# A DiT block on one core: keys loaded a group earlier, pairs of projection tiles leaving PSUM together, bias rows loaded at once, a longer lag behind the reciprocals

## The chip, the cores and the metric

The kernel runs on one core of one Trainium2 chip. The metric is the time of the program on the device in microseconds (us), as the median of several runs. The data type is float32 throughout.

## The reference

One block of a diffusion transformer with adaptive layer norm, for a batch of 2 sequences of 2048 tokens with 576 channels, 16 heads of 36 channels, and an MLP of 2304 hidden channels:

```
ada = silu(c) @ W_ada + b_ada                       # c (2, 576), W_ada (576, 3456)
shift_msa, scale_msa, gate_msa, shift_mlp, scale_mlp, gate_mlp = split(ada, 6)
h = layernorm(x) * (1 + scale_msa) + shift_msa      # x (2, 2048, 576)
q, k, v = split(h @ W_qkv + b_qkv, 3)               # W_qkv (576, 1728)
o = softmax(q * 36**-0.5 @ k.T) @ v                 # for each of the 16 heads
x = x + gate_msa * (o @ W_proj + b_proj)
h = layernorm(x) * (1 + scale_mlp) + shift_mlp
x = x + gate_mlp * (gelu_tanh(h @ W_fc1 + b_fc1) @ W_fc2 + b_fc2)
```

## The kernel before

The program has three stages: a front that makes queries, keys and values for all tokens; a loop over the attention of 8 blocks (a block is 512 queries of one sequence) times 16 heads, into which the projection and the MLP of earlier blocks are laid; and an end that finishes the projection and MLP of the last block. 576 channels are five pieces of the contraction, four of 128 and one of 64.

**The front** (up to L580). `load_ada` fetches the weights of one of the six parts of `ada`; `rows_of` (L408) multiplies them with the conditioning into two rows, and `modulation` (L428) turns these rows into columns, by five small matmuls, and adds 1 to the scales with three VectorE operations. For each of the 8 groups of 512 tokens, `queries_keys_values` (L206) loads four x tiles, normalizes them on VectorE, transposes them on TensorE, and applies scale and shift into `hT`. Then it makes the nine column tiles of 128 queries and keys. Two column tiles, a pair, share one PSUM tile `pq` of two banks (`wide`, of which there are three), one bank for each half, and the ninth is alone. The eviction `kept` (L255) adds the bias, on ScalarE for the first four column tiles and on VectorE for the others, and SP (SyncE's queue) stores the tile `ev` to `qk_d` in DRAM. In a pair it comes directly after the matmuls of its half. The values `pv` go through VectorE (`vt`, L342) and SP to `v_d`. The front's steps are generators; a second generator, `later` (L502), is advanced between them. It makes the two gates `g1` and `g2`, multiplies two bias rows of each sequence with them (tile `row`, L519 to L526, results in `gb_d` and `gp_d`), and multiplies the weights of the projection and of fc2 with them (`gated`: POOL loads at L480, VectorE multiplies at L493, POOL stores at L499).

**The loop.** A unit is one head of one block; there are 128. Its 2048 keys are taken in four groups, one to a slot of the loop, which has 512 slots. The work of one unit is spread over many slots, since scores run 8 slots ahead of the weighing (`AHEAD`):

- `load_keys` (L160): four SP loads, of keys `kT` (36 rows, twice) and queries `qT` (twice), at partitions 0 and 64; L169 and L170 issue them.
- `scores` (L625) on TensorE; `keep` (L638) copies them from PSUM to `e` on ScalarE; `maxima` (L643) folds them into `acc` on VectorE.
- After the fourth group, `turn` (L661) transposes the maxima on TensorE into the PSUM buffers that scores use; `across` reduces them (L671, `mx`), and SP stores them to `m_d` (L672) and loads them back broadcast over all partitions as `m` (L675).
- `less` (L680) subtracts `m` on VectorE, `exps` (L684) exponentiates on ScalarE, and `weigh` (L696) multiplies with the values `v` on TensorE. `load_values` (L600) fetches `v` with one SP load after a small VectorE memset.
- `take` (L708, L709) adds the two halves of the result into `up`; `store` sends it to `o_d` and `sum_d`: SP writes one half (L715, L716), POOL adds the other with accumulating DMAs (L717, L718).

In slot G the loop body issues, in this order: key and value loads, scores and copies, a filling, exponentials, transposes, the weighing, reductions and subtractions, and the stores of the unit that finished in the slot before. The loads are placed by these two conditions, in which `sg` and `g` are the group numbers of the scores' and the weighing's unit:

```
            if sg == 1 and su + 1 < NU:
                units[su + 1].load_keys()
            if g == 1 and -1 <= u and u + 1 < NU:
                units[u + 1].load_values()
```

With these, SP's order for one unit is m_d, m, o_d, sum_d, kT, qT, kT, qT, v.

A filling is a piece of work of an earlier block, chosen by a running account of cost. When a block's 16 heads are stored, its generators are queued: `gather` and `block`. `gather` (L1018) loads the sums and the outputs `oT` on POOL, takes the reciprocals of the sums and stores them to `rec_d` on POOL (L1040), then goes through KC + 2 steps: in step kc it loads the reciprocals of piece kc, broadcast over the rows of each head, by four or five SP loads (`r`, L1051) for each of the first four pieces, and multiplies piece kc - 2 of `oT` (L1059). `block` does the projection (`po`, L776), the residual, the second layer norm, fc1 (`pf`, L1147), gelu (L1158) and fc2 (`py`, L1195), whose result is added into `x_b` (L1207). A helper at L104 records the matmuls of the last contraction piece of 64 (`quads`), whatever the tile.

**The end** (L1365 to L1381) runs what is left after the last slot: each turn takes a filling and then calls `advance()` twice, which advances the gather of the last block by one step each time.

[...] SP's queue and ScalarE's queue issue hardware DMAs, POOL's issues software DMAs. The built program gives eight semaphores to SP's and ScalarE's transfers in turn, so that each issue also waits for the one eight before it.

Of the kernel before, what the change touches and what calls it, by code (L numbers as in the profile page):

```python
# [10 lines left out]
F32 = mybir.dt.float32  # L11
# [6 lines left out]
P = 128  # L18
# [4 lines left out]
def dit_block_kernel(  # L23
# [150 lines left out]
    with ExitStack() as front:  # L174
# [32 lines left out]
        def queries_keys_values(b, tb):  # L207
            mvs = lnp.tile([P, TB, nc.vector.BN_AGGR_DIM], F32, tag="mv", name=f"mv_{b}_{tb}", bufs=2)
            xts, xns = [], []
            for i in range(TB):  # L210
                xt = lnp.tile([P, C], F32, tag="xt", name=f"xt_{b}_{tb}_{i}", bufs=8)
                by = nc.sync if (b, tb) in ((0, 0), (0, 1)) else nc.scalar
                seq(by.dma_start(out=xt, in_=x[b, ts(tb * TB + i, P), :]))
                xts.append(xt)
            yield
# [52 lines left out]
            for m in range(0, NQK, 2):  # L268
                pq = wide(f"pq_{b}_{tb}_{m}")
                two = m + 1 < NQK  # L270
                for r in range(2):

                    cols, at = (ts(m + r, P), slice(None)) if two else (ts(m, P), ts(r, QB // 2))
                    n = QB if two else QB // 2
                    for kc in range(KC - 1):
                        seq(
                            nc.tensor.matmul(  # L277
                                pq[:, r, :n],
                                lhsT=w_in[:, kc, cols],
                                rhs=hT[:, kc, at],  # L280
                                start=(kc == 0 and not (two and r)),
                                stop=(kc == KC - 2 and two and r == 1),
                            )
                        )
                    if two and r == 0:
                        quads(
                            [pq[:, i, :] for i in range(2)],
                            [w_in[ts(i, 64), KC - 1, ts(m + i, P)] for i in range(2)],
                            tail,
                            (False, True),  # L290
                        )
                    if two:
                        kept(m + r, pq[:, r, :])
                        yield
                if not two:
                    quads(
                        [pq[:, i, :n] for i in range(2)],
                        [w_in[ts(i, 64), KC - 1, ts(m, P)] for i in range(2)],
                        [tail[i][:, ts(i, n)] for i in range(2)],
                        (False, False),  # L300
                    )
                    kept(m, pq[:, :, :n])
                    if tb == NQB - 1:
                        first_keys.extend(load_keys(0))
                    yield
# [91 lines left out]
            seq(nc.tensor.transpose(pt[:, ts(kc, B)], c_in[:, ts(kc, P)], ident[:B, :B]))  # L397
        cT = ap.tile([P, KC, B], F32, name="cT")
        seq(nc.vector.tensor_copy(cT.rearrange("p k b -> p (k b)"), pt[:, 0 : KC * B]))
        pt = bank("pt_bias")  # L400
        nb = NQK + NF
        seq(nc.tensor.transpose(pt[:, 0:nb], b_in, ident[:nb, :nb]))
        nq = C // P
        seq(nc.vector.tensor_scalar_mul(bias[:, 0:nq], pt[:, 0:nq], SCALE))
        seq(nc.vector.tensor_scalar_mul(bias[:, nq : nq + 1], pt[:, nq : nq + 1], qscale))
        seq(nc.vector.tensor_copy(bias[:, nq + 1 : nb], pt[:, nq + 1 : nb]))

        def rows_of(part):  # L408

            wa = was.pop(part)  # L410
# [17 lines left out]
        def modulation(part, t):  # L428

            pm = pms.pop(0) if pms else wide(f"pm_{part}")[:, 0, :]  # L430
            if part == 0:
                pms.append(pm[:, KC * B :])
            for fc in range(KC):
                m = P if fc < KC - 1 else KL
                seq(
                    nc.tensor.matmul(
                        pm[:m, ts(fc, B)], lhsT=t[:, ds(fc * P, m)], rhs=of_b, start=True, stop=True
                    )
                )
            to = 2 * (part // 3) + (1 - part % 3)  # L440
            add = 1.0 if part % 3 == 1 else 0.0
            spans = [(0, P, 0, KC - 1), (0, KL, KC - 1, KC), (64, KL, KC - 1, KC)]
            for at, m, lo, hi in spans:
                seq(
                    nc.vector.tensor_scalar_add(
                        mod[at : at + m, to, lo:hi, :].rearrange("p k b -> p (k b)"),
                        pm[:m, lo * B : hi * B],
                        add,
                    )
                )  # L450

        def gates(part, made):

# [48 lines left out]
        def later():  # L502

            was[2] = load_ada(2)
            was[5] = load_ada(5)
            yield
            yield
            yield
# [10 lines left out]
            half = [ap.tile([P, C], F32, name=f"half_{b}") for b in range(B)]  # L519
            for b in range(B):  # L520
                seq(nc.vector.tensor_scalar_mul(half[b], g2[b], 0.5))
                for to, src, g in ((gb_d, b_fc2, g2), (gp_d, b_proj, g1)):
                    r = ap.tile([1, C], F32, tag="row", name=f"row_{b}", bufs=2)
                    seq(nc.gpsimd.dma_start(out=r, in_=src.unsqueeze(0)))
                    seq(nc.vector.tensor_mul(r, r, g[b][0:1, :]))
                    seq(nc.gpsimd.dma_start(out=to[b].unsqueeze(0), in_=r))  # L526
            yield
            split = lambda w: [
                (pieces(w)[0][:, kc : kc + 2, :], P, 2) for kc in range(0, KC - 1, 2)
# [14 lines left out]
            t = rows_of(3)  # L544
            pas[4] = cleared(4)
            yield
            modulation(3, t)
            t = rows_of(4)
            yield
            modulation(4, t)  # L550

        next(stages[0])
        ts_ = [rows_of(part) for part in range(2)]
        next(stages[0])
        for part in range(2):
            modulation(part, ts_[part])
        for b in range(B):
            seq(nc.vector.tensor_copy(spread[b], of_b[:, b : b + 1].to_broadcast([P, P])))
        rest = later()
# [16 lines left out]
    with ExitStack() as main_part:  # L576
# [444 lines left out]
        def gather(k):  # L1021
# [18 lines left out]
            seq(nc.gpsimd.dma_start(out=flat_rows(rec_d[k]), in_=sums))  # L1040
            yield
            recs = []
            for kc in range(KC + 2):
                if kc < KC:
                    r = xp.tile([P, CP], F32, tag="xn", name=f"r_{k}_{kc}")[:, :QB]
                    for to in (0,) if kc < KC - 1 else (0, 64):
                        f, end = kc * P, min(kc * P + P, C)
                        while f < end:
                            n = min(D - f % D, end - f)
                            seq(  # L1050
                                nc.sync.dma_start(  # L1051
                                    out=r[ds(to + f - kc * P, n), :],
                                    in_=rec_d[k][f // D, :].partition_broadcast(n),
                                )
                            )
                            f += n
                    recs.append(r)
                if kc >= 2:
                    seq(nc.vector.tensor_mul(oT[:, kc - 2, :], oT[:, kc - 2, :], recs[kc - 2]))  # L1059
                yield  # L1060

        begun = {}
# [244 lines left out]
        for G in range(-AHEAD, NU * NG + 1):  # L1307
# [1 line left out]
            state["slot"] = G  # L1309

            su, sg = divmod(G + AHEAD, NG)
            if sg == 1 and su + 1 < NU:
                units[su + 1].load_keys()
            if g == 1 and -1 <= u and u + 1 < NU:
                units[u + 1].load_values()
            cu, cg = divmod(G - 1 + AHEAD, NG)
            chain = cg == NG - 1 and 0 <= cu < NU
# [50 lines left out]
        while work:  # L1368
# [8 lines left out]
                dones.append(lights.pop(0)()[1])  # L1377
            for done in dones:
                done()
            advance()  # L1380
            advance()  # L1381


# [43 lines left out]
```

## Time and profile before

| what | value |
|---|---|
| three runs | 3772.09, 3773.57, 3774.59 us; median 3773.57 |
| profiled execution, its own time | 3765.39 us |
| its span | 3763.6 us |
| granted TensorE clock, mean | 0.995 |
| PE (TensorE) busy | 3706.8 us |
| DVE (VectorE) busy | 2950.2 us |
| ACT (ScalarE) busy | 2331.1 us |
| POOL (GpSimd) busy | 617.1 us |
| moved by DMA | 382.11 MB, mean 102 GB/s |
| front, 0 to 262 us: PE busy | 232.6 us |
| loop, 262 to 3500 us: PE busy | 3219.6 us |
| end, 3500 to 3763.6 us: PE busy | 254.6 us |

The span is the time from the first to the last instruction of the profiled execution; its own time is 1.8 us more. In a row of waits, "PE s L625 <- DMA qT<-qk_d: 10.7, 5, 5.0" says that TensorE, before instructions of line 625 that write tile s, stood idle for 10.7 us in 5 places, at most 5.0 us at once, and that a DMA into qT from qk_d ended the wait. A row of the timeline has the start and the duration in us, the engine, the line, the operation, the tiles with partitions x elements, a count, and in brackets the idle time before it with what ended it. "SPq" and "DVEq" are the parts of an engine that issue transfers. The granted clock is the share of TensorE's full clock that the chip's throttle allowed.

### The profile page before, as it was taken

The numbers are of one execution on the slowest core, as the hardware profiler recorded it, in microseconds if no ns is written. First come the engines' busy times: TensorE is split into PE (matmuls) and PEld (weight loads), VectorE is DVE, ScalarE is ACT, GpSimd is POOL, SyncE is SP. The second block draws the span as 40 slices with busy tenths as digits, with TensorE's granted clock in tenths as the row PEclk, the third lists the DMA queues.
The fourth block names the chain that finished last, engine by engine and source line by source line (L and its number), as shares of the span: only waits on it lengthen the run. The fifth ranks groups of instructions, "written<-read, shape, count | busy, mean of one in ns | idle before, by whom it ended". The sixth has DMA issues, their size and how long they took to land. (4 is left out here: it accounts for less than half of the span.)

```text
span 3763.6 us, 59194 instructions
## 1 busy us (share of the span) xinstructions
PE 3706.8 (98%) x23926; PEld 1727.1 (46%) x23926; DVE 2950.2 (78%) x3002; ACT 2331.1 (62%) x2164; POOL 617.1 (16%) x868
## 2 busy tenths in 40 slices
PE   8999999999999999999999999999999999999999
PEld 4454443534444534444444444444445444444465
DVE  4626889879888888898889888988889888988322
ACT  0005777668776686667677767767766766676321
POOL 0201111221111121211121112111121112111211
PEclk9999999999999999999999999999999999999999
DMA  6823444454435353534353535434353435343422
GB/s 211 287 101 94 97 91 101 110 132 100 78 81 118 73 104 75 129 69 101 76 116 82 115 66 118 97 75 95 77 122 69 99 77 116 77 93 71 123 75 69
DMA packets 426864, 382.11 MB, mean 102 GB/s; under 512 B 313734, under 2 KB 314776, under 8 KB 426592
## 3 DMA queue, kind: packets, MB, share of 16 engines
q1 hardware_dynamic: 354912, 180.02, 24.1%
q0 software_dynamic: 69952, 194.77, 18.7%
q8 instruction: 189, 3.10, 0.4%
q10 hardware_dynamic: 1728, 3.54, 0.3%
q14 instruction: 83, 0.68, 0.1%
HBM read 306.98 MB, written 71.21 MB: 100 GB/s over the span
## 5 line engine op out<-in xcount | busy, mean ns | idle before, releaser
L638 ACT COPY e<-s 128x1024 f32<-128x1024 f32 x1024 | 990.1, 1024 | 723.4 <-PE s L625 721.7
L680 DVE TENSOR_TENSOR e<-e,m 128x2048 f32<-128x2048 f32 x512 | 1162.2, 2276 | 8.6 <-DMA m<-m_d 8.6
L643 DVE TENSOR_TENSOR acc<-acc,e 128x1024 f32<-128x1024 f32 x768 | 939.5, 1223 | 185.2 <-ACT e L638 142.0
L684 ACT ACTIVATE e<-e 128x2048 f32<-128x2048 f32 x512 | 991.1, 1936 | 9.1 <-DVE e L680 9.1
L625 PE MATMUL s<-qT,kT 36*64 36x512 f32 x8192 | 984.2, 592 | 11.8 <-DMA qT<-qk_d 10.7
L696 PE MATMUL av<-e,v 64*64 64x512 f32 x8192 | 978.6, 593 | 0.0
L1195 PE MATMUL py<-w,gT 128*128 128x288 f32 x2304 | 584.4, 412 | 0.0
L625 PEld LDWEIGHTS s<-qT,kT 36*64 36x64 f32 x8192 | 312.8, 133 | 577.8 <-issue 535.1
L696 PEld LDWEIGHTS av<-e,v 64*64 64x64 f32 x8192 | 297.9, 133 | 518.0 <-issue 463.9
L1147 PE MATMUL pf<-h_b,w_b 128*128 128x512 f32 x1152 | 532.3, 606 | 0.0
L1195 PEld LDWEIGHTS py<-w,gT 128*128 128x128 f32 x2304 | 434.0, 191 | 179.5 <-issue 41.3
L717 POOL DMA_DIRECT2D o_d<-up x128 | 109.6, 856 | 2089.2 <-DMA o_d<-up 1252.1
L1147 PEld LDWEIGHTS pf<-h_b,w_b 128*128 128x128 f32 x1152 | 208.4, 190 | 320.2 <-issue 309.1
L671 DVE TENSOR_REDUCE mx<-mt 128x4 f32<-128x512 f32 x128 | 88.3, 690 | 184.9 <-PE mt L661 184.9
L1158 ACT ACTIVATE gT<-pf,bias 128x512 f32<-128x512 f32 x144 | 99.1, 688 | 204.6 <-PE pf L104 134.6
L1167 DVE SCALAR_TENSOR_TENSOR th<-th,gT 128x1024 f32<-128x1024 f32 x72 | 88.1, 1223 | 99.4 <-ACT th L1165 99.4
L643 DVE TENSOR_TENSOR acc<-e 128x1024 f32<-128x1024 f32 x128 | 155.6, 1215 | 4.4 <-ACT e L638 4.4
L718 POOL DMA_DIRECT2D sum_d<-up x128 | 143.5, 1121 | 0.9 <-issue 0.9
L1207 DVE TENSOR_TENSOR x_b<-py,x_b 128x288 f32<-128x288 f32 x192 | 81.1, 452 | 78.6 <-PE py L1195 78.5
L277 PE MATMUL pq<-hT,w_in 128*128 128x512 f32 (+1 forms) x320 | 130.6, 560 | 10.6 <-ACT ev L261 6.9
L776 PE MATMUL po<-wpr_p,oT 128*128 128x288 f32 x512 | 132.6, 412 | 0.0
L743 POOL DMA_DIRECT2D w_b<-in_L_cond_W_fc_dram x72 | 68.3, 949 | 299.6 <-PE pf L1147 269.7
(157 smaller groups left out, 2361.3 us busy)
## 6 DMA issues: line engine op xcount, KB each, us to landing
w<-w_d POOLq DMA_DIRECT2D x72, 576.0 KB, 5.8
v<-v_d SPq DMA_DIRECT2D x128, 296.0 KB
kT<-qk_d SPq DMA_DIRECT2D x256, 144.0 KB
w_b<-in_L_cond_W_fc_dram POOLq DMA_DIRECT2D x72, 512.0 KB, 4.6
m<-m_d SPq DMA_DIRECT2D x128, 256.0 KB
qT<-qk_d SPq DMA_DIRECT2D x256, 72.0 KB
w_d<-wg POOLq DMA_DIRECT2D x12, 864.0 KB, 5.4
qk_d<-ev SPq DMA_DIRECT2D x36, 256.0 KB
```

Of the source, the lines that this page charges most:

```text
L277: nc.tensor.matmul(pq[:, r, :n], lhsT=w_in[:, kc, cols], rhs=hT[:, kc, at], start=(kc == 0 and not (two and r)), stop=(kc == KC - 2 and tw ...
L625: nc.tensor.matmul(s[ts(c, 64), i, :], lhsT=self.kT[at, ds((2 * g + j) * P + 64 * c, 64)], rhs=self.qT[at, :], start=True, stop=True,)
L638: seq(nc.scalar.copy(self.es[g][:, j], s))
L643: top = lambda out, x, y: seq(nc.vector.tensor_max(out, x, y))
L680: seq(nc.vector.tensor_sub(e, e, m))
L684: seq(nc.scalar.activation(e, e, AF.Exp))
L696: nc.tensor.matmul(self.av[ts(i, 64), r, :], lhsT=self.v[ts(r, 64), ds((c + i * (HALF // P)) * HA, 64)], rhs=e[ts(r, 64), j, i, :], start= ...
L717: seq(nc.gpsimd.dma_start(out=o, in_=hi[1:HA, :], accum_op=ALU.add))
L718: seq(nc.gpsimd.dma_start(out=sums, in_=hi[0:1, :], accum_op=ALU.add))
L776: nc.tensor.matmul(outs[n][:, :C2], lhsT=src[:, kc, ts(i, P)], rhs=w_[:, kc, ts(n, C2)], start=(kc == 0), stop=False,)
L1147: nc.tensor.matmul(pfs[j], lhsT=wc[:, kc, ts(j, P)], rhs=h2[:, kc, :], start=(kc == 0 and j == 0), stop=(kc == KC - 2 and j == 1),)
L1195: nc.tensor.matmul(py[n][:, :C2], lhsT=gTs[f - f % 2][:, f % 2, ts(i, P)], rhs=w2s[f - f % 2][:, f % 2, ts(n, C2)], start=(j == 0), stop=( ...
```

## The change

Seven edits.

1. The x tiles of the very first group of 512 tokens are loaded by ScalarE's queue, no longer by SP.
2. In the front's pairs both evictions come after the matmuls of both halves.
3. The transposition of the biases (`pt_bias`) and its three VectorE operations move behind the first two modulations; `modulation` now returns its VectorE part as a function, so that the matmuls of both modulations come ahead of the VectorE operations of both.
4. The four bias rows (of fc2 and of the projection, for each sequence) are loaded at the start of `later` by POOL into one tile `lines`, on partitions 0, 32, 64 and 96, and multiplied in place there with the same partition of the gate.
5. `gather` has KC + 3 steps: a piece of `oT` is multiplied three steps after its reciprocals are loaded.
6. Keys of the next unit are loaded when `sg == 0` and values when `g == 0`. SP's order for one unit becomes kT, qT, kT, qT, v, m_d, m, o_d, sum_d, and the memset of `v` moves directly behind the `up` addition on VectorE.
7. In the end each turn advances by one or two steps in alternation (`1 + state["slot"] % 2`) instead of two.

The order of the matmuls on TensorE is the same except for the bias transposition. In the end, VectorE's `x_b` additions of the third fc2 product come to stand ahead of the first and second products with the reciprocals.

```diff
--- before.py
+++ after.py
@@ -209,7 +209,7 @@
             xts, xns = [], []
             for i in range(TB):
                 xt = lnp.tile([P, C], F32, tag="xt", name=f"xt_{b}_{tb}_{i}", bufs=8)
-                by = nc.sync if (b, tb) in ((0, 0), (0, 1)) else nc.scalar
+                by = nc.sync if (b, tb) == (0, 1) else nc.scalar
                 seq(by.dma_start(out=xt, in_=x[b, ts(tb * TB + i, P), :]))
                 xts.append(xt)
             yield
@@ -289,10 +289,13 @@
                             tail,
                             (False, True),
                         )
-                    if two:
+                    if two and r == 0:
+                        yield
+                if two:
+                    for r in range(2):
                         kept(m + r, pq[:, r, :])
-                        yield
-                if not two:
+                    yield
+                else:
                     quads(
                         [pq[:, i, :n] for i in range(2)],
                         [w_in[ts(i, 64), KC - 1, ts(m, P)] for i in range(2)],
@@ -397,14 +400,6 @@
             seq(nc.tensor.transpose(pt[:, ts(kc, B)], c_in[:, ts(kc, P)], ident[:B, :B]))
         cT = ap.tile([P, KC, B], F32, name="cT")
         seq(nc.vector.tensor_copy(cT.rearrange("p k b -> p (k b)"), pt[:, 0 : KC * B]))
-        pt = bank("pt_bias")
-        nb = NQK + NF
-        seq(nc.tensor.transpose(pt[:, 0:nb], b_in, ident[:nb, :nb]))
-        nq = C // P
-        seq(nc.vector.tensor_scalar_mul(bias[:, 0:nq], pt[:, 0:nq], SCALE))
-        seq(nc.vector.tensor_scalar_mul(bias[:, nq : nq + 1], pt[:, nq : nq + 1], qscale))
-        seq(nc.vector.tensor_copy(bias[:, nq + 1 : nb], pt[:, nq + 1 : nb]))
-
         def rows_of(part):
 
             wa = was.pop(part)
@@ -440,14 +435,18 @@
             to = 2 * (part // 3) + (1 - part % 3)
             add = 1.0 if part % 3 == 1 else 0.0
             spans = [(0, P, 0, KC - 1), (0, KL, KC - 1, KC), (64, KL, KC - 1, KC)]
-            for at, m, lo, hi in spans:
-                seq(
-                    nc.vector.tensor_scalar_add(
-                        mod[at : at + m, to, lo:hi, :].rearrange("p k b -> p (k b)"),
-                        pm[:m, lo * B : hi * B],
-                        add,
+
+            def done():
+                for at, m, lo, hi in spans:
+                    seq(
+                        nc.vector.tensor_scalar_add(
+                            mod[at : at + m, to, lo:hi, :].rearrange("p k b -> p (k b)"),
+                            pm[:m, lo * B : hi * B],
+                            add,
+                        )
                     )
-                )
+
+            return done
 
         def gates(part, made):
 
@@ -503,6 +502,11 @@
 
             was[2] = load_ada(2)
             was[5] = load_ada(5)
+            lines = ap.tile([P, C], F32, name="lines")
+            for b in range(B):
+                for i, src in enumerate((b_fc2, b_proj)):
+                    at = ds(64 * b + 32 * i, 1)
+                    seq(nc.gpsimd.dma_start(out=lines[at, :], in_=src.unsqueeze(0)))
             yield
             yield
             yield
@@ -519,11 +523,10 @@
             half = [ap.tile([P, C], F32, name=f"half_{b}") for b in range(B)]
             for b in range(B):
                 seq(nc.vector.tensor_scalar_mul(half[b], g2[b], 0.5))
-                for to, src, g in ((gb_d, b_fc2, g2), (gp_d, b_proj, g1)):
-                    r = ap.tile([1, C], F32, tag="row", name=f"row_{b}", bufs=2)
-                    seq(nc.gpsimd.dma_start(out=r, in_=src.unsqueeze(0)))
-                    seq(nc.vector.tensor_mul(r, r, g[b][0:1, :]))
-                    seq(nc.gpsimd.dma_start(out=to[b].unsqueeze(0), in_=r))
+                for i, (to, g) in enumerate(((gb_d, g2), (gp_d, g1))):
+                    at = ds(64 * b + 32 * i, 1)
+                    seq(nc.vector.tensor_mul(lines[at, :], lines[at, :], g[b][at, :]))
+                    seq(nc.gpsimd.dma_start(out=to[b].unsqueeze(0), in_=lines[at, :]))
             yield
             split = lambda w: [
                 (pieces(w)[0][:, kc : kc + 2, :], P, 2) for kc in range(0, KC - 1, 2)
@@ -544,16 +547,24 @@
             t = rows_of(3)
             pas[4] = cleared(4)
             yield
-            modulation(3, t)
+            modulation(3, t)()
             t = rows_of(4)
             yield
-            modulation(4, t)
+            modulation(4, t)()
 
         next(stages[0])
         ts_ = [rows_of(part) for part in range(2)]
         next(stages[0])
-        for part in range(2):
-            modulation(part, ts_[part])
+        for done in [modulation(part, ts_[part]) for part in range(2)]:
+            done()
+        pt = bank("pt_bias")
+        nb = NQK + NF
+        seq(nc.tensor.transpose(pt[:, 0:nb], b_in, ident[:nb, :nb]))
+        nq = C // P
+        seq(nc.vector.tensor_scalar_mul(bias[:, 0:nq], pt[:, 0:nq], SCALE))
+        seq(nc.vector.tensor_scalar_mul(bias[:, nq : nq + 1], pt[:, nq : nq + 1], qscale))
+        seq(nc.vector.tensor_copy(bias[:, nq + 1 : nb], pt[:, nq + 1 : nb]))
+
         for b in range(B):
             seq(nc.vector.tensor_copy(spread[b], of_b[:, b : b + 1].to_broadcast([P, P])))
         rest = later()
@@ -1040,7 +1051,8 @@
             seq(nc.gpsimd.dma_start(out=flat_rows(rec_d[k]), in_=sums))
             yield
             recs = []
-            for kc in range(KC + 2):
+            LAG = 3
+            for kc in range(KC + LAG):
                 if kc < KC:
                     r = xp.tile([P, CP], F32, tag="xn", name=f"r_{k}_{kc}")[:, :QB]
                     for to in (0,) if kc < KC - 1 else (0, 64):
@@ -1055,8 +1067,9 @@
                             )
                             f += n
                     recs.append(r)
-                if kc >= 2:
-                    seq(nc.vector.tensor_mul(oT[:, kc - 2, :], oT[:, kc - 2, :], recs[kc - 2]))
+                if kc >= LAG:
+                    c = kc - LAG
+                    seq(nc.vector.tensor_mul(oT[:, c, :], oT[:, c, :], recs[c]))
                 yield
 
         begun = {}
@@ -1309,9 +1322,9 @@
             state["slot"] = G
 
             su, sg = divmod(G + AHEAD, NG)
-            if sg == 1 and su + 1 < NU:
+            if sg == 0 and su + 1 < NU:
                 units[su + 1].load_keys()
-            if g == 1 and -1 <= u and u + 1 < NU:
+            if g == 0 and -1 <= u and u + 1 < NU:
                 units[u + 1].load_values()
             cu, cg = divmod(G - 1 + AHEAD, NG)
             chain = cg == NG - 1 and 0 <= cu < NU
@@ -1377,8 +1390,9 @@
                 dones.append(lights.pop(0)()[1])
             for done in dones:
                 done()
-            advance()
-            advance()
+            state["slot"] += 1
+            for _ in range(1 + state["slot"] % 2):
+                advance()
 
 
 # ---- launch: one core; inputs and outputs as the reference has them ----
```

## The prediction

> **What bounds the kernel now.** I read the page's busy shares first, then what TensorE waited for, then the granted clock in small windows, then two stretches of the timeline.
>
> ```profile
> PE 3706.8 (98%) x23926; PEld 1727.1 (46%) x23926; DVE 2950.2 (78%) x3002; ACT 2331.1 (62%) x2164; POOL 617.1 (16%) x868
> ```
>
> TensorE works through 98% of the span; only 56.8 us of 3763.6 are idle, so no edit off TensorE's path can be worth more than the idle time that it ends, and the slow clock behind it. The idle time by cause (total us, times, longest; two lines for the pairs of the front):
>
> ```profile
> PE s L625 <- DMA qT<-qk_d: 10.7, 5, 5.0
> PE pq L277 <- ACT ev L261: 6.9, 8, 1.2
> PE pf L104 <- DVE x_b L1207: 5.6, 1, 5.6
> PE pv L104 <- DVE vt L342: 3.0, 1, 3.0
> PE pq L277 <- DVE ev L263: 2.0, 2, 1.0
> ```
>
> The keys wait falls at 770, 2763 and 3171 us, each time where a block's reciprocals are loaded. An idle stretch also costs what follows it; windows (length, PE, PEld, DVE, ACT, POOL busy, granted clock, DMA share, GB/s):
>
> ```profile
> 94.50:98.50 4.00, 3.48 (x14) 2.08 (x15) 1.93 (x8) 0.00 (x0) 2.43 (x4) 0.57 0.59 131
> 774.00:784.40 10.40, 9.11 (x21) 2.75 (x22) 9.33 (x8) 6.23 (x5) 0.74 (x2) 0.51 0.62 164
> 2767.40:2774.20 6.80, 6.76 (x19) 3.16 (x20) 6.66 (x7) 4.33 (x4) 0.00 (x0) 0.50 0.51 143
> 3173.60:3183.80 10.20, 10.17 (x28) 4.75 (x25) 8.45 (x7) 4.74 (x5) 0.00 (x0) 0.50 0.45 102
> 3555.80:3562.70 6.90, 5.12 (x8) 1.80 (x9) 4.14 (x8) 0.00 (x0) 0.00 (x0) 0.51 0.31 88
> ```
>
> After stalls of 5.0, 3.3, 2.2 and 5.6 us the clock stood at half for 10.4, 6.8, 10.2 and 6.9 us. The waits of 0.8 to 1.2 us in the front leave it at 1.00.
>
> Where the keys wait comes from (SP's issues, block 0), and the end's stall:
>
> ```profile
> 763.44 1.48 SPq L1051 DMA_DIRECT2D r<-rec_d  x4
> 765.03 0.34 SPq L672 DMA_DIRECT2D m_d<-mx  x1
> 768.52 0.34 SPq L675 DMA_DIRECT2D m<-m_d  x1
> 769.71 1.89 SPq L1051 DMA_DIRECT2D r<-rec_d  x5
> 771.69 2.29 DVE L680 TENSOR_TENSOR e<-e,m 128x2048 f32<-128x2048 f32 x1 [0.15 <-DMA m<-m_d]
> 771.73 0.29 SPq L169 DMA_DIRECT2D kT<-qk_d  x1
> 775.06 1.97 PE L625 MATMUL s<-qT,kT 36*64 36x512 f32 x4 [4.96 <-DMA qT<-qk_d]
> ...
> 3551.56 0.69 DVE L1059 TENSOR_TENSOR oT<-oT,r 128x512 f32<-128x512 f32 x1 [14.84 <-DMA r<-rec_d]
> 3556.46 0.69 DVE L1059 TENSOR_TENSOR oT<-oT,r 128x512 f32<-128x512 f32 x1 [4.21 <-DMA r<-rec_d]
> 3557.07 0.81 DVE L1207 TENSOR_TENSOR x_b<-py,x_b 128x288 f32<-128x288 f32 x2
> 3557.58 1.97 PE L104 MATMUL pf<-h_b,w_b 64*64 64x512 f32 x4 [5.65 <-DVE x_b L1207]
> ```
>
> SP stands at the first reciprocal row until rec_d has landed (763.44). The maxima, more rows and only then the keys follow. The first kT goes out 0.04 us after the maxima have landed: eight semaphores serve SP's transfers in turn, and the maxima are eight issues back.
>
> **The change, part by part.**
>
> *Pairs in the front.* The second half's matmuls of a pair no longer wait for the first half's eviction. Ten waits in the pairs, 6.9 + 2.0 = 8.9 us, go. Both evictions (0.69 us each on ACT, 0.75 to 0.81 on DVE) now follow the pair; the next pair takes another of three PSUM buffers and runs 8.1 us, which covers 1.6 us. Where VectorE's part also waits behind a weight scaling (1.95 us) it is still covered; uncovered, each of 16 pairs would cost 0.8. -8.9.
>
> *Rows of biases.* Four 0.75 us products on VectorE wait for their rows, 9.2 us for the b_proj rows and 2.3 for one b_fc2 row, since POOL issues each load behind the store before it. Behind them stand the value evictions L342, and behind these TensorE (3.0). All four loads now lie at 3 us, next to free; the four products take 3.0 us, at 79 to 83. The half clock cost the 16 matmuls that follow 5.1 us instead of 4.15. -3.0 - 0.95 = -4.0. POOL's weight loads L480 also leave some 11 us earlier; nothing on the path waits for them.
>
> *Start.* Four x loads go to ACT's queue and SP's ada loads start 1.8 us sooner. The row: DMA share 0.92 over the first 20 us, 278 GB/s; TensorE's first ada product waits until 11.4. [...] x may land some 3.7 us later (estimate: 512 packets at half the rate of 165 per us that the trace shows); its transposes wait anyway until 19.6, when ada's products end, and normalized x was ready at 16.1. The moved bias transpose (0.28 on PE, three DVE operations 0.37 together) now delays the first hT by about 0.2, and the dropped wait between the two modulations (0.5) pays for that. I take 0, from -1.8 to +2.
>
> *Reciprocals in three steps, the end.* VectorE's two x_b additions of the third product now stand ahead of the first oT product. That product and the next held them for 14.84 + 4.21 us. The first x_b pair can run when its matmuls end at 3541.5, so L104 goes on at 3551.9: -5.65. Half the clock until 3562.7 slowed the work from 3557.6, 5.1 us of it, so -2.5 more, less 0.3 for the modelled edges. The next stall would be po (L776), which needs the last product: its row lands at 3560.9, VectorE has it done by 3562, and po now starts near 3564.7 instead of 3572.7. -7.9. One advance fewer in every other turn of the last loop changes no other engine's order.
>
> *Keys ahead of the maxima, the seven blocks in the loop.* Let T be the moment at which SP gets past rec_d (763.44, 1154.31, 2754.67, 3162.56 for blocks 0, 1, 5, 6). Four rows take 1.5; then come four key issues (1.65) and v (0.45), so that kT is out at T+1.6 and landed by about T+4.5; TensorE wants it at T+6.7 (block 0) to T+13. The keys stall goes. But m_d now leaves at T+3.6 instead of T+1.5, and behind v. The row: v's 2048 packets of 148 bytes end 4.0 to 7.2 us after its issue. [...] No run here shows m_d right behind v; I take 4, as POOL's queue is quiet there.
>
> What stands behind m: VectorE's subtraction (2.28), then x_b (0.45 for the first bank), which frees the PSUM of TensorE's next filling. Block 5: m 2762.35 to 2766.35, subtraction to 2768.65, bank free at 2769.1; scores now run on time, 2763.1 to 2764.9, and TensorE then stands 4.2 us. Before, the filling began at 2771.05, all at half clock. Now 2769.1, with some 3 us of half clock behind it: it ends at 2778.0 instead of 2778.5. Block 6: bank at 3176.5, filling over near 3185 instead of 3187. Block 0: the maxima's transposes need both the acc chain (subtraction, product, subtraction, two acc, one half acc: 9 us after m at 775.8, 784.5) and ACT's copy, which waits for the sum_d stores (10.2 us after o_d's issue); 784.7 instead of 786.1, but the half clock reaches further: +1 in all. Blocks 1 to 4 have 4 us more room (bank at T+14.7, wanted at T+14.8): 0. Sum -0.5 - 1.9 + 1 = about -1: **one stall takes the other's place**. Ends: -24 (no stall left) to +15 (2 us more in each of seven).
>
> *Keys in the other 121 units.* Keys and v leave when the last unit's L696 ends; mx follows 5.3 to 7.0 us (median) later, and v ends by 1.6 + 5.25 = 6.9. m_d is late by 1.6 at worst. Subtraction begins 7.7 us (median) after m's issue, m lands after 3.2 to 4.3: some 4 us to spare. The memset of v (0.08) now follows the `up` sum, which needs the same matmuls. 0; each microsecond past that room costs 121.
>
> **Sum.** -8.9 - 4.0 + 0 - 7.9 - 1 = -21.8. The profiled execution takes 3765.39 (span 3763.6); it becomes 3743.6. The runs' median is 8.2 above it, so 3773.57 - 21.8 = 3751.8; I say 3752.
>
> **Rivals.** *The lead of the keys pays in full*: the three stalls go and nothing comes instead. For it: each is put down to qT. Against: VectorE already waits for m in these places (8.6 us, 8 times), so m has no room. Stalls 10.5 us and half of the 27.2 us of slow clock that work ran in: -24 instead of -1, 3729. *The late maxima cost more*: 2 us more in each of seven blocks, 3767. *The front is held by its transfers*: at 120 to 160 us the DMA share is 0.93; the pairs' gain then halves and the end stays: 3757 to 3762. *Slower*: v beside m_d in every unit eats the 4 us to spare. If the subtraction comes later by d on average, 3752 + 121 d; the sign turns at d = 0.18 us, and 0.4 gives 3800. For it: the unit with least room starts its subtraction 3.2 us after m's issue; against: VectorE is idle 22%.
>
> **How the numbers follow.** Stall for stall, 3752: 0.52, on its own 3745 to 3760. Full lead 0.08; late maxima 0.15; held front 0.10; slower 0.15. The range reaches from part of the full lead to past the late maxima, and into the slower case while its d is under 0.17, 3738 to 3772, which leaves out most of the first and the last. Within 0.2% (7.5 us, about what a measurement tells from no change) falls part of the late maxima. Faster 0.78, same 0.07, slower 0.15.
>
> **What would show it.** Right: no wait of L277 for ev; no wait of a row product; L104 near 3551 on an x_b already done, no half clock there; at the reciprocals TensorE waiting on x_b or ACT's copies instead of qT, DVE's wait for m grown from 8.6 to some 30 us. Wrong: a clock of 1.00 through blocks 0, 5 and 6; DVE waiting for m in ordinary units; pv or hT waits grown in the front.

## The result, and the profile after

The changed kernel takes 3736.36 us (median of five runs, 3735.96 to 3738.32) against 3772.09 us (median of five, 3769.88 to 3774.59): a ratio of 0.991, 95% interval 0.9899 to 0.9921. It is faster, by 35.7 us in the medians where 21.8 had been worked out, and its median lies 1.6 us below the low end of the forecast range, 3738.

The profiled execution after took 3736.07 us (span 3734.3). The one of before, 3765.39, was a quick one: beside the experiments the kernel before was timed 48 times more, in three sets with medians of 3768.7 to 3771.3. The two traces therefore differ by 29.3 us only, and by that part of the gain the steps can be read one by one. The page after:

```profile
PE 3692.3 (99%) x23926; PEld 1724.1 (46%) x23926; DVE 2947.2 (79%) x3002; ACT 2329.2 (62%) x2164; POOL 616.2 (17%) x868
```

TensorE is idle for 42.0 us instead of 56.8 and busy for 14.5 us less, with the same 23926 matmuls. So half of the 29.3 us is not idle time: 13.4 us of the shorter busy time lies at the five places (about 92 us, blocks 0, 5 and 6, the end) behind which the clock stood at half before. What TensorE waited for now (total us, times, longest):

```profile
PE mt L672 <- DVE acc L654: 8.7, 2, 8.0
PE py L1208 <- DVE x_b L1220: 6.3, 2, 3.8
PE pt_c L400 <- ACT c_in L397: 4.9, 1, 4.9
PE pa L411 <- DMA wa<-in_L_cond_W_ada_dram: 4.1, 1, 4.1
PE pt L237 <- DVE hT L156: 4.0, 8, 0.6
PE pt_bias L562 <- ACT hT L154: 1.5, 1, 1.5
```

The waits for `ev`, for `vt` and for `qT` are gone, and so is the wait of L104 for `x_b` in the end. In the place of the keys stalls stand one of 8.0 us at block 0, where the transposes of the maxima (`mt`) wait for VectorE, and two at blocks 5 and 6 (3.8 and 2.6 us), where fc2 (`py`) waits for PSUM that VectorE's `x_b` addition frees. VectorE was late, in both, because it had waited for the maxima and less for the reciprocals at the products. Before:

```profile
DVE oT L1059 <- DMA r<-rec_d: 42.2, 11, 14.8
...
DVE e L680 <- DMA m<-m_d: 8.6, 8, 3.5
```

After:

```profile
DVE e L691 <- DMA m<-m_d: 58.8, 10, 11.6
...
DVE oT L1072 <- DMA r<-rec_d: 17.0, 4, 11.9
```

The granted clock after these stalls, and in the end (length, PE, PEld, DVE, ACT, POOL busy, granted clock, DMA share, GB/s):

```profile
760.70:770.94 10.24, 4.65 (x24) 1.92 (x28) 10.10 (x11) 6.20 (x6) 2.08 (x4) 0.50 0.82 201
2752.50:2757.50 5.00, 4.99 (x11) 3.56 (x12) 4.90 (x5) 4.76 (x5) 0.00 (x0) 0.50 0.62 171
3157.60:3163.68 6.08, 6.07 (x13) 4.36 (x14) 5.94 (x6) 5.43 (x5) 0.00 (x0) 0.50 0.62 172
3520.00:3545.00 25.00, 24.99 (x85) 12.95 (x84) 6.34 (x10) 4.08 (x6) 5.81 (x10) 1.00 0.67 185
```

At block 0 the clock was at half for 10.2 us, but 5.6 of them fell into the stall itself; at blocks 5 and 6 it held TensorE's work for 5.0 and 6.1 us, where it had been 6.8 and 10.2. In the end there is no slow clock any more.

### The profile page after: what moved, and what is told of

Same layout as the page of the kernel before. It is cut to its first block, busy times and chain, and to the rows that moved or that the text cites. A ratio compares the mean times of both kernels' runs of the same rounds, so it can differ in the third digit from the quotient of the medians.

```text
span 3734.3 us, 59188 instructions
## 1 busy us (share of the span) xinstructions
PE 3692.3 (99%) x23926; PEld 1724.1 (46%) x23926; DVE 2947.2 (79%) x3002; ACT 2329.2 (62%) x2164; POOL 616.2 (17%) x868
## 3 DMA queue, kind: packets, MB, share of 16 engines
q10 hardware_dynamic: 2304, 4.72, 0.4%
## 5 line engine op out<-in xcount | busy, mean ns | idle before, releaser
L691 DVE TENSOR_TENSOR e<-e,m 128x2048 f32<-128x2048 f32 x512 | 1161.7, 2274 | 58.8 <-DMA m<-m_d 58.8
L636 PE MATMUL s<-qT,kT 36*64 36x512 f32 x8192 | 974.0, 589 | 1.5 <-PE pv L327 1.0
L277 PE MATMUL pq<-hT,w_in 128*128 128x512 f32 (+1 forms) x320 | 131.8, 564 | 1.5 <-DVE hT L156 1.5
```

Of the source, the lines that this page charges most:

```text
L277: nc.tensor.matmul(pq[:, r, :n], lhsT=w_in[:, kc, cols], rhs=hT[:, kc, at], start=(kc == 0 and not (two and r)), stop=(kc == KC - 2 and tw ...
L636: nc.tensor.matmul(s[ts(c, 64), i, :], lhsT=self.kT[at, ds((2 * g + j) * P + 64 * c, 64)], rhs=self.qT[at, :], start=True, stop=True,)
L691: seq(nc.vector.tensor_sub(e, e, m))
```

## The steps of the gain, in the traces and alone

Since TensorE's matmuls stand in the same order in both kernels (but for the bias transposition), the start of each can be compared with its start before. The shift is -1.6 us at 41 us, falls by 4.7 between 91 and 99 us, where the bias rows had held the values, and reaches -17.0 when the loop begins. It is -20.4 at the end of the loop and -29.3 at the last matmul. The third column has each edit alone, put into the kernel before:

| part | predicted | in the traces | alone: ratio, 95% interval | alone, us |
|---|---|---|---|---|
| pairs (edit 2) | -8.9 | -10.7 | 0.9973, 0.9962 to 0.9984 | -10.2 |
| rows of biases (4) | -4.0 | -4.7 | 0.9988, 0.9979 to 0.9997 | -4.5 |
| start (1, 3) | 0 | -1.6 | 0.9993, 0.9984 to 1.0002 | -2.6 |
| lag and end (5, 7) | -7.9 | -8.9 | 0.9972, 0.9961 to 0.9983 | -10.6 |
| keys and values (6) | -1 | -3.4 | 0.9984, 0.9975 to 0.9993 | -6.0 |
| sum | -21.8 | -29.3 | | -33.9 |

The last column is the ratio times the median of before of the same set (3771.26 or 3769.61). The parts add, as near as such intervals can tell: the five ratios together take off 0.0090, and so does the whole.

## The experiments

**The four parts beside the keys, each alone in the kernel before.** Each is cut out of the change's diff as it stands there; its main lines are shown. The pairs, edit 2:

```diff
-                    if two:
+                    if two and r == 0:
+                        yield
+                if two:
+                    for r in range(2):
                         kept(m + r, pq[:, r, :])
-                        yield
-                if not two:
+                    yield
+                else:
```

> The kernel before with the pairs' evictions after both halves (edit 2 alone). By the prediction's step -8.9: some 3761 against 3770, no wait of L277 for ev. By the rival that transfers hold the front: half of it, -4.5, with other waits grown in the front. The traces of before and after put steps of 10.7 us in all beside the pairs.

Measured 3760.11 us against 3771.26. No wait of L277 is left in its trace, and by the loop's begin TensorE is 10.2 us ahead of the trace of before. The rival that transfers hold the front is refuted.

The rows of biases, edit 4:

```diff
+            lines = ap.tile([P, C], F32, name="lines")
...
+                    seq(nc.gpsimd.dma_start(out=lines[at, :], in_=src.unsqueeze(0)))
...
-                    seq(nc.vector.tensor_mul(r, r, g[b][0:1, :]))
+                    seq(nc.vector.tensor_mul(lines[at, :], lines[at, :], g[b][at, :]))
```

> The kernel before with the bias rows loaded at once (edit 4 alone). By the prediction's step -4.0: some 3766, no wait of a row product, no stall of TensorE behind vt near 92 us and no slow clock behind it; the traces of before and after put 4.7 us there. If the stall at 92 us and its slow clock differ from execution to execution, the spread of the runs (3765.6 to 3773.9 before) shrinks with them.

Measured 3766.16. The stall behind `vt` is gone. The runs still spread over 3761.68 to 3770.19, so this place does not make the spread alone.

The start, edits 1 and 3:

```diff
-                by = nc.sync if (b, tb) in ((0, 0), (0, 1)) else nc.scalar
+                by = nc.sync if (b, tb) == (0, 1) else nc.scalar
...
-            modulation(part, ts_[part])
+        for done in [modulation(part, ts_[part]) for part in range(2)]:
+            done()
+        pt = bank("pt_bias")
```

> The kernel before with four x loads on ScalarE's queue and the bias transposition after the modulations (edits 1 and 3 alone). By the prediction 0 (-1.8 to +2); the traces of before and after show 1.6 us gained by 41 us.

Measured 3768.88, which its interval does not tell from no change. Its traces say more: in the six profiles with the old start TensorE's first ada product began at 10.9 to 12.2 us, in the eight with the new start at 9.5 to 10.4. Some of the lead is lost again between 21 and 25 us, where the moved bias transposition waits 1.5 us for ScalarE's first `hT`, the first pair 1.5 us more, and the clock goes to half (for 6.83 us from 23.4 us in the trace after, for 3.41 in that of before).

The lag and the end, edits 5 and 7:

```diff
-            for kc in range(KC + 2):
+            LAG = 3
+            for kc in range(KC + LAG):
...
-            advance()
-            advance()
+            state["slot"] += 1
+            for _ in range(1 + state["slot"] % 2):
+                advance()
```

> The kernel before with three steps of lag behind the reciprocals and alternating advances in the end (edits 5 and 7 alone). By the prediction -7.9: some 3762, no stall of L104 for x_b near 3552 and a clock of 1.00 there; the traces of before and after put 8.9 us there. If the slow clock of the end varies from execution to execution, the spread of the runs shrinks too.

Measured 3759.15, with no wait of L104 for `x_b`. VectorE's wait for `m` is 36.4 us already here, four times that of before: with three steps of lag the product with the reciprocals no longer stands ahead of the subtraction, and the same lateness is put down to the maxima.

**The keys, taken back and alone.**

```diff
-            if sg == 0 and su + 1 < NU:
+            if sg == 1 and su + 1 < NU:
                 units[su + 1].load_keys()
-            if g == 0 and -1 <= u and u + 1 < NU:
+            if g == 1 and -1 <= u and u + 1 < NU:
                 units[u + 1].load_values()
```

> The changed kernel with keys and values loaded at group 1 again (edit 6 taken back alone). Theory A (one stall takes the other's place): the traces of before and after differ by 3.4 us in the loop, so this kernel is slower than the changed one (3736.4) by about that, 3740, the keys stalls come back at blocks 0, 5 and 6 and the waits for the maxima shrink from 58.8 us to about 9. Theory B (edit 6 carries more than the one profiled execution shows, since the runs of before lie 4 to 9 us above its profiled execution and those of after do not): 3745 or more.

> The kernel before with edit 6 alone. Theory A: 3772 - 3.4 = 3769, within 0.2% of before. Theory B: 3762 to 3764. In both VectorE's wait for m grows to some 55 us and no wait of scores for qT is left.

Taken back (the diff above, in the changed kernel): 3738.42 us, ratio to before 0.9921 (0.9909 to 0.9934). So edit 6 is worth some 2 us there by the medians and some 4 by the two ratios (0.9910 and 0.9921), which is nearer to theory A. Alone in the kernel before (the same lines the other way): 3764.32 against 3769.61, some 6 us, which is nearer to theory B; but its interval (2.6 to 9.4 us) holds A's 3.4 as well, so the times do not decide between the two. TensorE's waits are those that were expected: taken back,

```profile
PE s L636 <- DMA qT<-qk_d: 11.5, 4, 5.3
```

and alone, no wait for `qT`, but

```profile
PE py L1195 <- DVE x_b L1207: 8.7, 2, 4.5
PE mt L661 <- DVE acc L643: 8.1, 2, 7.4
```

So edit 6 alone exchanges 10.2 us of stalls (before) for 16.2, and is still 3.1 us faster over the loop in the traces. What it saves is slow clock: the clock stood at half for 6.8 us at each of the three blocks, where the trace of before has 10.2, 6.8 and 10.2, and TensorE worked 15.4 us in it instead of 25.9. How much that is differs between executions, and 2 to 6 us is as near as these runs come. VectorE's wait for `m` was 37.0 us in both kernels. That misses both expectations, 55 for edit 6 alone and about 9 with it taken back: edit 5 brings as much of the 58.8 us as edit 6 does.

**What holds the maxima back.** SP's issues at block 0 after:

```profile
743.81 1.48 SPq L1063 DMA_DIRECT2D r<-rec_d  x4
745.34 0.33 SPq L169 DMA_DIRECT2D kT<-qk_d  x1
...
746.52 0.47 SPq L170 DMA_DIRECT2D qT<-qk_d  x1
750.46 0.39 SPq L617 DMA_DIRECT2D v<-v_d  x1
750.95 1.23 SPq L683 DMA_DIRECT2D m_d<-mx  x1
754.24 0.33 SPq L686 DMA_DIRECT2D m<-m_d  x1
```

The keys are out at 746.5 and v only at 750.46, and the store of the maxima is behind it.

```diff
-            if g == 0 and -1 <= u and u + 1 < NU:
+            if g == 1 and -1 <= u and u + 1 < NU:
                 units[u + 1].load_values()
```

> The changed kernel with only the values loaded at group 1 again, the keys stay at group 0, so that the store of the maxima no longer stands behind v. If v, whose issue waits for the last weighing to end, is what makes the maxima late (block 0: keys out at 746.5, v only at 750.46, the maxima at 750.95), the maxima leave some 4 us earlier; the stalls of 3.75 and 2.58 us at blocks 5 and 6 and their slow clock (2.5 + 3.3) go and half of the 8.0 us at block 0: about 3720. If the reciprocal rows alone make the maxima late, no change: 3736.

Measured 3725.89 (ratio 0.9883, 0.9869 to 0.9896): some 10 us better than the changed kernel, from a single line. The maxima's store left 2.5 us earlier at block 0, counted from SP's passing the first row (4.6 us after it instead of 7.1), 0.8 at block 5 and 0.5 at block 6, and the stalls fell at blocks 0 (8.0 to 4.7 us) and 5 (3.8 to 1.2), but hardly at block 6 (2.6 to 2.5):

```profile
PE mt L672 <- DVE acc L654: 6.2, 4, 4.7
...
PE py L1208 <- DVE x_b L1220: 3.7, 2, 2.5
```

At blocks 5 and 6 no slow clock followed them. The cause that the expectation names was not the right one, though: v did not wait for the weighing. What SP waited for at 740 to 775 us, in the changed kernel:

```profile
SPq L1063 <- DMA rec_d<-sums: 28.2, 1, 28.2
SPq L617 <- DMA r<-rec_d: 6.7, 2, 3.4
```

v stood behind the first reciprocal row, eight issues back in the turn of semaphores, and without v ahead of it the maxima's store waited 1.4 us for the same row. The first line is the root: SP stood 28.2 us at the first row. It did so before the change too, at all eight blocks:

```profile
SPq L1051 <- DMA rec_d<-sums: 227.0, 8, 29.7
```

**Taking the root away.** One more step between the store of the reciprocals and the first load of their rows:

```diff
             seq(nc.gpsimd.dma_start(out=flat_rows(rec_d[k]), in_=sums))
             yield
+            if k < NB - 1:
+                yield
```

> The changed kernel with one further step between the store of the reciprocals and the first load of their rows, in all blocks but the last, so that SP no longer stands at the first row until the reciprocals have landed; the order on TensorE is the same. If that stand is the root of both kinds of stall, those of 8.0, 3.75, 2.58 and 0.47 us go, and 8.1 us of slow clock behind them: 3736.4 - 22.9 = 3713.5, no wait of the subtraction for m above 4 us. Rival: the rows are then late for the last product and the projection waits for it: 3736 or slower, with a wait of L787 for oT.

Measured 3717.05 (0.9857, 0.9842 to 0.9872), 3.5 us over the number expected. SP's stand at the rows fell from 234.7 us in all (changed kernel) to 34.3, of which 27.6 are the last block's. The stalls at blocks 5 and 6 and their slow clock are gone, the projection doesn't wait for its last product, and the stall at block 0 is 2.5 us. There the subtraction still waits 6.8 us for `m`, where at most 4 was expected. That rest has another cause:

```profile
732.11 1.08 SPq L617 DMA_DIRECT2D v<-v_d  x1
737.03 1.12 SPq L683 DMA_DIRECT2D m_d<-mx  x1
750.54 0.33 SPq L686 DMA_DIRECT2D m<-m_d  x1
```

Here SP waits for no row, and the store of the maxima takes 13.5 us to land, behind v.

The next kernel has this edit and that of `values_back`.

> The changed kernel with one further step ahead of the rows and the values back at group 1, the keys at group 0. In rows_step_later the maxima's store at block 0 took from 737.0 to 750.5 behind v, whose packets trickled from 735 to 749 beside the projection's weights. If the order in the queue holds it, it lands within some 4 us and the 2.5 us stall of the transposes goes: 3717 - 3 = 3714. If the weights' traffic alone holds it, 3717.

Measured 3713.57 (0.9855, 0.984 to 0.9869). Without v ahead of it the same store landed in 6.6 us:

```profile
737.13 0.34 SPq L683 DMA_DIRECT2D m_d<-mx  x1
743.77 0.34 SPq L686 DMA_DIRECT2D m<-m_d  x1
```

That is half, not the 4 us expected. What remains falls together with POOL's adding of the block's x tiles (512 packets of 2304 bytes, from 736 to 744 us); the packets of the projection's weights, which the expectation names, start only at 743 us. The stall at block 0 is 1.3 us, and no slow clock follows it. The two kernels' intervals overlap, so that it is the trace, and not the time, that shows this gain.

The next has it with that of `keys_undone`.

> The changed kernel with one further step ahead of the reciprocal rows and without edit 6: keys and values at group 1, behind the maxima. If SP's stand at the first row is the root, edit 6 has nothing left to cure: as fast as with edit 6, 3717, no wait of scores for qT, and, since v no longer stands ahead of the maxima's store, no wait of the transposes of 2.5 us at block 0: 3712 to 3717. If the keys' lead has a worth of its own, the keys waits stay at 5 us or more: 3725 or above.

Measured 3718.66 (0.9867, 0.9851 to 0.9882; runs from 3714.71 to 3721.55), a little above the 3712 to 3717 expected. There is no wait for `qT` above 0.6 us, and at block 0 none of the transposes; the 0.6 us there was still followed by 3.4 us of half clock. Against `rows_step_later` the lead of keys and values is worth 1.6 us in the medians. Against `rows_step_later_values_back`, which was timed in the same set and differs in the keys' condition alone, the keys' lead is worth 5.1 us. Both are less than the runs of this kernel spread (6.8 us), and the two profiled executions took the same time (3715.89 and 3716.13), so that a small worth of the lead is neither shown nor excluded.

The last of them adds to `rows_step_later_values_back`:

```diff
-            LAG = 3
+            LAG = 3 if k < NB - 1 else 4
```

> The former kernel, with four steps of lag instead of three for the last block, so that VectorE's last x_b additions stand ahead of the first oT product in the end. In rows_step_later TensorE waited there 1.4 us for x_b. With the wait gone: 1.4 less than the former kernel, some 3712; if the last product is then late for the projection, slower than the former by the wait of L787.

Measured 3713.02 (0.9853, 0.9837 to 0.9869; runs from 3712.56 to 3713.70). The wait of 1.3 us for `x_b` in the end is gone, but the medians differ by 0.6 us only, which the runs do not tell from nothing. It is the best version: 23.3 us below the changed kernel's median (of an earlier set), 55.7 below that of the kernel before in its set (3768.7). What TensorE waits for in it begins with the front, and every wait of the loop is below 1.2 us:

```profile
PE pt_c L400 <- ACT c_in L397: 5.1, 1, 5.1
PE pa L411 <- DMA wa<-in_L_cond_W_ada_dram: 4.2, 1, 4.2
PE pt L237 <- DVE hT L156: 4.0, 8, 0.6
PE pt_b L851 <- DVE x_b L1222: 2.4, 6, 0.4
PE mt L672 <- DVE acc L654: 1.9, 2, 1.1
```

**The kernel before, profiled again.**

> The kernel before, unchanged, profiled once more. The profiled execution of before was 3765.4, its other runs 3764 to 3779. If the stalls differ in length from execution to execution, another profile puts its difference at the keys stalls of blocks 0, 5 and 6, in the first 100 us and at the end, and nowhere else.

It took 3766.64 us. Against the first trace it is 0.9 us late by 125 us, gains 0.2, 0.5 and 0.6 at blocks 0, 1 and 5, loses 1.5 at block 6 and 0.1 at the end, and nothing elsewhere. Of these places only block 1 had not been named. With 3766.6 it is no typical execution either; the profile of `start_only` (3773.07) is: the same places, keys stalls of 12.9 us in all and more slow clock behind them. The 48 timed runs say the same by their mean granted clock: 0.995 in those of 3761.5 to 3766.7 us, 0.994 from 3765.6 to 3770.3, 0.993 from 3768.0 to 3776.7 and 0.992 in the two slowest, 3776.7 and 3779.3.

## Why the prediction was right, and where it fell short

*The likeliest case*, stall for stall, is what happened: the keys stalls went and waits behind late maxima came, on the engine and the lines that were named. Counted from SP's passing the first row, the maxima were to be in VectorE's hands at T+12.4, 11.7 at blocks 0 and 5; they were at T+14.1 and 11.8. At block 5 a stall of 4.2 us was worked out, and 3.75 measured. The 4 us by which the maxima were taken to be late were an estimate that no run shows as such: counted from the same point, the subtraction began 5.8, 4.8, 4.2 and 4.0 us later than in the kernel before at blocks 0, 1, 5 and 6. At block 5 the maxima's store landed at T+8.7, and the load behind it needed 3.1 us.

*Keys, -1 predicted, -3.4 in the traces: the mis-sized term is the slow clock.* By blocks, -0.5, -1.9 and +1 were worked out for 5, 6 and 0; the traces have -1.6, -2.8 and -0.4, and small losses in two other places. Over the same matmuls around blocks 0, 5 and 6 TensorE's idle time grew by 2.8, 0.5 and 0.4 us, and its busy time fell by 3.2, 2.1 and 3.2. At block 5 the prediction lets the filling begin 1.95 us earlier and last 1.4 longer; counted from the same matmuls ahead of the block, it began 2.5 earlier and lasted 0.9 longer. Nor had it run before "all at half clock": the half clock ended at 2774.2 us, 3.2 us into a filling of 7.5. At block 0 the late v (T+6.6, where T+3.2 was taken) is the step that failed: the turn of eight semaphores was used to explain why the keys were late, and not applied to v, which then stood in the same place. The stall grew by it, but 5.6 of the 10.24 us of half clock fell into the stall, in which TensorE ran nothing. One ordinary unit lost 1.2 us at 925 us: its maxima's store took 8.3 us to land (3.7 before), as its packets started only from 911 to 913 us, behind those of v, which moved from 905 to 913 beside a load on POOL's queue, and ScalarE's copy of `up` came 2.3 us late behind it. This is the slower case in one place; the other 120 units had the slack that was worked out.

*v ahead of the maxima's store:* at block 0 all 128 packets of the maxima's store start in the microsecond in which v's last of 2048 do (from 753.0 us), and in `rows_step_later` the store landed 13.5 us after its issue against 6.6 without v ahead. At blocks 1, 5 and 6 the store took 4.4, 4.7 and 4.1 us where before it took 1.7, 2.1 and 1.6. But v is not all of it: in `values_back`, with only the keys ahead, it took 3.0 us at block 5 and 4.2 at block 6.

*Pairs, -8.9 predicted, -10.7:* the ten waits went as counted. What was left out is 1.7 us: the transposes of the next 512 tokens (L237) waited 4.65 us in three places for `hT` behind the evictions, and 2.95 now.

*Rows, -4.0 predicted, -4.7*: right. *The end, -7.9 predicted, -8.9*: right, with the stall and the slow clock gone and no new wait; po starts 8.9 us earlier where 8.0 was worked out.

*Start, 0 predicted, -1.6:* the 1.8 us by which SP's ada loads start sooner were counted as nothing. That 0 was the author's estimate, and no run shows it as such: in the traces the first ada product began 1.8 us earlier (at 9.58 us instead of 11.40), by just what SP's first three ada loads were issued sooner (at 1.17, 1.64 and 2.23 us instead of 3.00, 3.47 and 4.07). The prediction's row has the DMA engines busy 0.92 of the first 20 us; but in the first 5 us before the change they were busy for 0.57 only, and 1.02 (full) in the next 5, so that there was room at the very start.

*The rest of the gap*, 6.4 us between the traces' 29.3 and the medians' 35.7, is the kernel before's profiled execution. The prediction took the 8.2 us by which the median lay above it for a constant that the change keeps. It was the price of stalls that were longer, or had more half clock behind them, in other executions, as the granted clock of the 48 runs shows, and most of it went with the stalls: after the change the median lies 0.3 us above the profiled execution.

*The rivals.* The full lead is refuted (14.3 us of new stalls); late maxima that cost more in all seven blocks too: blocks 2 to 4 show VectorE waiting 4.4 to 5.4 us for `m` and TensorE not at all, block 1 0.3 us. VectorE's wait for `m` was forecast at some 30 us and measured 58.8. The 21.5 us of it at blocks 1 to 4 did next to no harm, since those four blocks had the room that was given them. The held front did not come, and the slower case in one unit only.

## What to carry to other kernels

In the kernel before, SP's queue stood for up to 29.7 us at a row whose reciprocals had not landed, what came behind it paid, and moving one victim ahead made the next one the victim: edit 6 was worth 2 to 6 us, and letting the late transfer be issued one step later some 19. Ask what the queue stands at before choosing what to move past it. A stall's price here was its idle time and the slow clock behind it (2.19 and 10.24 us at block 6 of the kernel before), so compare what the same matmuls cost in busy time, and take a single profile's distance to the median for stalls that vary, not for a constant.

## What was not expected of the hardware

The half clock came in stretches of equal size. In the clock records of all fourteen profiles (they begin at 13 to 20 us) every stretch of half clock, but for the one at the very end, lasted 3.41, 6.83, 10.24 or 13.65 us, one to four times 3.41. In the table the number does not follow from the length of the stall (us of idle time, then us of half clock):

```
place                     kernel          idle   half clock
values, about 92 us       before          3.02   3.41
values, about 92 us       start_only      3.82   6.83
block 0                   before          4.96   10.24
block 0                   keys_undone     5.32   13.65
block 0                   after           7.96   10.24
block 5                   before          3.08   6.83
block 5                   start_only      3.53   10.24
block 5                   keys_undone     1.89   3.41
block 6                   before          2.19   10.24
block 6                   after           2.58   6.83
block 6                   values_back     2.47   none
front, about 196 us       rows_only       0.87   3.41
front, about 203 us       before          0.87   none
block 0                   (1)             0.59   3.41
end                       before          5.65   6.83
end                       pairs_only      5.97   10.24

(1) rows_step_later_keys_undone
```

Two of them as windows of the trace, of `keys_undone` and of `start_only` (columns as above):

```profile
2751.46:2754.87 3.41, 3.41 (x9) 2.41 (x8) 3.27 (x6) 3.41 (x4) 0.00 (x0) 0.50 0.42 141
```

```profile
2771.15:2781.39 10.24, 9.73 (x27) 4.67 (x24) 8.08 (x7) 4.46 (x5) 0.00 (x0) 0.50 0.49 105
```

The half clock followed idle times of 1.89, 0.87 and 0.59 us too, and at block 5 of `start_only` the clock stayed at half for 10.24 us, three times 3.41, of which TensorE was busy for 9.73. What decides whether a short wait is followed by half clock, and whether for 3.41 us or for three times that, these runs do not show. Each 3.41 us in which TensorE works at half the clock costs some 1.7 us (an estimate: half of 3.41, since matmuls of fc2 at block 6 of before follow each other at 0.48 us in it and at 0.24 after it). So four such places can spread the runs by several us: the kernel before ran from 3761.53 to 3779.31 us over all sets, the best version, whose profile has half clock at the start and in the last 0.4 us alone, from 3712.56 to 3713.70 in its four runs.
